# Gathers behind the accumulating transfers, an earlier first expert slot, and another layout of the list operand

## The chip, the cores and the metric

The kernel runs on one core of a Trainium2 chip. What counts is the device time of one execution in microseconds (us), the median of several runs. A profiled execution gives the page and the trace from which every time here is read; all durations are us unless marked ns. The engines are PE (TensorE: PE for matmuls, PEld for its weight loads), DVE (VectorE), ACT (ScalarE), POOL (GpSimd) and SP (SyncE, which here only issues DMAs). "L1404" is line 1404 of the kernel before.

## The reference

The input is an image of 256 channels and 64 x 64 = 4096 tokens. Layer 0 adds a linear attention over windows. Layer 1 adds softmax attention with 8 heads, then a routed feed-forward network with 8 experts of which every token uses two:

```python
# x: (1, 256, 64, 64)
x = x + _L0_conv_ref(_gn(x), Wq, Wk, Wv, Wout, bout)     # linear attention in windows
t = _to_tokens(x)                                        # (1, 4096, 256)
t = t + _L1_attn_ref(_ln_t(t), w_qkv, b_qkv, w_out, b_out)
t = t + _L1_ffn_ref(_ln_t(t), Wr, br, ln_g, ln_b, W1, b1, W2, b2)

# _L1_ffn_ref, xt of shape (4096, 256), 8 experts, hidden size 1024
probs = softmax(xt @ Wr + br)
top_p, top_idx = top_k(probs, 2)
weights = top_p / top_p.sum(-1, keepdims=True)
xe = layernorm(xt) * ln_g[e] + ln_b[e]
y[e] = gelu(xe @ W1[e] + b1[e]) @ W2[e] + b2[e]
out = sum over the two chosen experts e of weight[e] * y[e]
```

## The kernel before

The first part (to about 1105 us) is layer 0 and the projections of queries, keys and values. The change does not touch it.

**Attention (1105 to 2210).** There are 16 rounds, one for each chunk of 512 queries and each half of the heads. Each round runs over 32 key tiles `i`. For a tile, `scores` makes eight score matmuls (L1739) into one PSUM bank (`ps_one`, the first of four heads) and three banks (`ps_three`). ScalarE takes the exponential of the first bank (L1748) and of the three others (L1751) into one of eight SBUF buffers `pe`. `value_sums` multiplies the buffer by the values (L1698). The softmax denominators need the sum of a round's 32 buffers. For most tiles VectorE adds the buffer to a running total (L1770). Seven tiles of a round (i = 5, 9, ... 29; five in the last round) go another way: GpSimd starts an accumulating DMA (L1759) that adds the buffer to a second total. The buffer is free for a later tile once that transfer has landed; the list `free` gives it out again six tiles on. Later in the next round the totals are joined, turned and divided, and `some_projections` (L1673, L1677) makes the output projection of finished tokens.

**Early slots.** The experts work in slots of up to 256 tokens (two units of 128). For four experts the first slot can be filled from the first twelve token tiles, whose routing is done during the attention; the token lists of these early slots, `lists`, come back from DRAM in round 12. A slot has these steps, all in the generator `run`, which yields after each piece so that other work can be laid between the pieces:

- `load`: the weights through SP (`weights`, L1350 to L1375), and for each unit an indirect gather of 128 token rows issued by GpSimd (L1389).
- `enter`: four transposes by TensorE (L1404) into the bank `ps_tp`, and two operations that scale and shift them into `xe`. For the early slots those are ScalarE's (L1409); for the others VectorE's (L1413).
- eight hidden tiles: two matmuls each (L1438) into `ps_hp`, and GELU by ScalarE (L1441).
- for each unit the output product (L1454, eight matmuls into `ps_yp`), an addition of the bias (L1458) and an indirect scatter by GpSimd (L1459).

fp32 matmuls have two records each in the trace, transposes and bf16 matmuls one.

The loop over the attention's tiles calls `next(work_on)` twice in the last round: the first call loads slot 0, the second slot 1. A gather waits for its list and stands in GpSimd's queue where the scheduler put it, which is round 12, among the accumulating transfers. [...]

**End of the attention.** After the last tile the code adds the last denominators (`by_ones` into `den`), copies the last sums (`take`, L1782 on ScalarE), takes four reciprocals (L1894) and products (L1895) on VectorE, and makes the last projections (L1673). The PSUM banks of the attention are then given up, and `route_and_run` opens its own.

**`route_and_run` (L1473 to L1664).** It finishes the routing of all tokens on VectorE while TensorE works on early slots: `advance(n)` takes n pieces of `run`. It counts tokens by expert with two matmuls (L1533, L1534), works out the row of each token in its expert's list, and then inverts these positions into a list of tokens for each slot, by matmuls with one-hot operands. This list stage works on 8 token tiles at a time (`G`), in four groups for the first choice and four for the second. VectorE makes `line` (L1633), the one-hot of the place within a unit, 128 places for each of 8 tiles; and `piece` with three planes for the 72 units (`NPC`): the one-hot of the unit (L1635), that times the token's number (ScalarE, L1636), and that times a tile number `high` (L1637). Eight matmuls (L1639) follow with `line` as weights and the last two planes of `piece` as the moving operand, 144 columns. `line` and `piece` have two buffers each, and one piece of an early slot (`advance(1)`) is laid behind every group. The operand `counter`, 0 to 127 repeated 8 times, is made on GpSimd (L1621), and `high` too (L1629). After the last group VectorE turns the sums into `source` (L1656 on) and the usual slots' gathers can start.

The operands before have the tile index last:

```python
line  = r_work.tile([P, P, G], BF16)          # weights  line[:, :, i]
piece = r_work.tile([P, 3, NPC, G], BF16)     # moving   piece[:, 1:, :, i]
```

so that both operands of a matmul step through SBUF by 8 elements, 16 bytes.

## Time and profile before

| what | us |
|---|---|
| median of 3 runs (2773.73 to 2778.75) | 2773.91 |
| the profiled execution | 2777.12 |
| its span in the trace | 2775.3 |
| mean granted TensorE clock | 0.986 |
| attention, 16 rounds | about 1105 to 2210 |
| four early slots, with the list stage (2252 to 2277) | 2218 to 2290 |
| usual slots | 2290 to 2730 |
| last combination and output | 2730 to 2775 |

How to read it: a timeline row gives the start, the length, the engine, the line, the operation and its operands as output<-input, the shape, the number of instructions, and in brackets the idle time of the engine ahead of it with what ended it. Several like instructions in succession share a row. The DMA queue's own time is not in an engine's row: a transfer issued by GpSimd shows there only with its issue. In the rows by stretch, PEclk is the share of full speed granted to TensorE. Pages of the costliest groups put the attention's matmuls first, with L1739 at 564.2 and 558.0 us and L1698 at 352.5 and 193.9; the experts' products L1438 and L1454 have 249.7 and 241.0. The list's matmuls L1639 have 18.0 in the stretch from 2252 to 2278, in 64 records.

### The profile page before, as it was taken

The page shows a single profiled execution, that of the slowest core. Times are in us where ns is not written, and L with a number is a line of the kernel's source. Part 1 is how long each engine was busy: PE and PEld are TensorE (multiplying, and loading weights), DVE is VectorE, ACT ScalarE, POOL GpSimd, SP SyncE. Part 2 cuts the span into 40 slices and gives each one's busy share as a digit, 9 for nine tenths or more (in the row PEclk, how much of TensorE's full clock was granted, in tenths as well). Part 3 has the DMA queues.
Part 4 walks back from the last instruction along what each step waited for, and adds up shares of the span by engine and source line. Part 5 has one row for each costly group of instructions (what it writes and reads, how often), then busy time and mean ns, then how long its engine had stood idle before and what let it go on. Part 6 is the DMA issues. An engine that isn't in the chain of part 4 may idle for free.

```text
span 2775.3 us, 72311 instructions
## 1 busy us (share of the span) xinstructions
PE 2661.1 (96%) x31106; PEld 1212.8 (44%) x31106; DVE 1873.0 (67%) x2517; ACT 1512.8 (55%) x2110; POOL 822.4 (30%) x918
## 2 busy tenths in 40 slices
PE   6889999988999999999999999999999999999996
PEld 5454336645433655111212121212121278888884
DVE  6758688565878875888888889888788851111114
ACT  3322323222332334999898989898889742222222
POOL 2057777404777741000000100000200012222220
PEclk9999999999999999999999999999999999999996
DMA  5000000000000000555555555555556546565665
GB/s 144 6 23 25 11 28 21 8 12 23 24 11 28 21 21 1 107 111 118 108 120 109 121 112 112 111 112 123 117 109 150 142 132 196 200 208 190 217 207 194
DMA packets 120995, 266.09 MB, mean 96 GB/s; under 512 B 20658, under 2 KB 81816, under 8 KB 106580
## 3 DMA queue, kind: packets, MB, share of 16 engines
q0 software_dynamic: 22368, 133.18, 23.0%
q1 hardware_dynamic: 91124, 119.20, 13.1%
q10 hardware_dynamic: 7168, 8.92, 1.0%
q8 instruction: 248, 4.06, 0.6%
q14 instruction: 87, 0.71, 0.1%
HBM read 127.81 MB, written 18.12 MB: 53 GB/s over the span
## 4 chain that ended last, share of the span: by engine, by line
PE 91%; DMA 3%; DVE 3%; issue 2%; POOL 1%; ACT 0%; ACTq 0%; SPq 0%; DVEq 0%; POOLq 0%
PE ps_three L1739 18%; PE ps_acc L1698 18%; PE ps_hp L1438 8%; PE ps_sc L822 8%; PE ps_yp L1454 8%; PE ps_acc L838 7%; PE ps_sc L722 3%; PE ps_sc L749 3%; PE ps_acc L780 3%; PE ps_two L407 2%; PE ps_two L440 2%; PE ps_mm L1238 2%; DMA yrows<-v,qk 2%; PE ps_two L521 1%; PE ps_acc L768 1%
## 5 line engine op out<-in xcount | busy, mean ns | idle before, releaser
L1739 PE MATMUL ps_three<-qk 32*64 32x512 f32 x6144 | 564.2, 613 | 2.3 <-DVE t L1677 1.3
L1739 PE MATMUL ps_one<-qk 32*64 32x512 f32 x2048 | 558.0, 614 | 5.2 <-ACT pe L1748 5.2
L642 ACT COPY sm<-ps_sc 128x384 f32<-128x384 f32 (+3 forms) x454 | 218.5, 511 | 525.7 <-PE ps_sc L822 338.7
L1770 DVE TENSOR_TENSOR act<-act,pe 128x2048 f32<-128x2048 f32 x195 | 446.8, 2292 | 84.9 <-ACT pe L1751 53.0
L1751 ACT ACTIVATE pe<-ps_three 128x1536 f32<-128x1536 f32 x330 | 477.4, 1447 | 0.0
L649 DVE TENSOR_TENSOR sm<-ps_sc,mask 128x512 f32<-128x512 f32 (+3 forms) x740 | 340.2, 519 | 68.9 <-PE ps_sc L822 65.7
L1770 DVE TENSOR_TENSOR act<-act 128x2048 f32<-128x2048 f32 x150 | 344.9, 2299 | 57.2 <-ACT act L1751 44.0
L649 POOL TENSOR_TENSOR sm<-sm,mask 128x192 f32<-128x192 f32 (+3 forms) x428 | 349.7, 847 | 113.9 <-ACT sm L642 113.6
L1759 POOL DMA_DIRECT2D pe<-pe x108 | 93.1, 862 | 933.1 <-ACT pe L1751 653.5
L1698 PE MATMUL ps_acc<-pe,v 128*32 128x512 f32 x2640 | 352.5, 606 | 0.0
L1441 ACT ACTIVATE v<-ps_hp,qk 128x256 f32<-128x256 f32 (+1 forms) x288 | 133.1, 462 | 343.8 <-PE ps_hp L1438 341.9
L1739 PEld LDWEIGHTS ps_three<-qk 32*64 32x64 f32 x6144 | 112.6, 130 | 415.4 <-ACT pe L1748 243.2
L1751 ACT ACTIVATE act<-ps_three 128x1536 f32<-128x1536 f32 x182 | 263.1, 1446 | 0.0
L1438 PE MATMUL ps_hp<-qk 128*128 128x256 f32 (+1 forms) x1152 | 249.7, 373 | 0.3 <-ACT qk L1409 0.3
L1454 PE MATMUL ps_yp<-qk,v 128*128 128x256 f32 x1088 | 241.0, 379 | 0.0
L822 PE MATMUL ps_sc<-qk 32*64 32x384 f32 (+3 forms) x3584 | 234.5, 458 | 0.1
L1748 ACT ACTIVATE pe<-ps_one 128x512 f32<-128x512 f32 x330 | 197.4, 598 | 66.5 <-PE ps_one L1739 36.1
L649 POOL TENSOR_TENSOR sm<-sm,ycut 128x384 f32<-128x384 f32 (+4 forms) x146 | 147.3, 1029 | 252.3 <-ACT sm L642 252.0
L1438 PEld LDWEIGHTS ps_hp<-qk 128*128 128x128 f32 x1152 | 197.2, 190 | 47.4 <-ACT v L1441 13.1
L1454 PEld LDWEIGHTS ps_yp<-qk,v 128*128 128x128 f32 x1088 | 204.2, 190 | 26.5
L838 PE MATMUL ps_acc<-sm,v 128*32 128x256 f32 (+3 forms) x2688 | 213.2, 419 | 0.1
L1698 PE MATMUL ps_acc<-act,v 128*32 128x512 f32 x1456 | 193.9, 604 | 0.0
(335 smaller groups left out, 2875.4 us busy)
## 6 DMA issues: line engine op xcount, KB each, us to landing
pe<-pe POOLq DMA_DIRECT2D x108, 1024.0 KB, 7.6
qk<-in_L_ffn_W SPq DMA_DIRECT2D x72, 1024.0 KB
by<-recs SPq DMA_DIRECT2D x48, 256.0 KB
qk<-in_L_ffn_b SPq DMA_DIRECT2D x36, 128.0 KB
rows<-in_x SPq DMA_DIRECT2D x16, 256.0 KB
y<-yrows SPq DMA_DIRECT2D x8, 512.0 KB
y<-yrows ACTq DMA_DIRECT2D x8, 512.0 KB
rec<-recs SPq DMA_DIRECT2D x60, 64.0 KB
```

The source lines that it names most:

```text
L642: copied = nc.scalar.copy(sm[:, :used], sc[:, :used])
L649: done = engine.tensor_mul(to, of, mk.unsqueeze(1).to_broadcast(list(to.shape)))
L822: nc.tensor.matmul(scs[h][u : u + rows, at : at + n], kT[hs[h], P * i + u : P * i + u + rows], qT[hs[h], CH * ix + CELL * c0 : CH * ix + C ...
L838: nc.tensor.matmul(acc[hs[h], CELL * c0 : CELL * c1], v[:, i, hs[h]], sms[h][:, at : at + n], start=not begun[0], stop=last and at == plac ...
L1438: nc.tensor.matmul(hp[:, :n], w1[:, k, tok(m)], x_now[:, k, :n], start=k == 0, stop=k == KC - 1)
L1441: done["gelu"] = nc.scalar.activation(hid[:, m, :n], hp[:, :n], AF.Gelu, bias=cols[:, m : m + 1]).ins
L1454: product = nc.tensor.matmul(yp, hid[:, m, tok(j)], w2[:, m, :], start=m == 0, stop=m == NH - 1)
L1698: nc.tensor.matmul(to[D * hd : D * (hd + 1), :], lhsT(hd), rhs(hd), start=start, stop=stop, skip_group_check=True,)
L1739: nc.tensor.matmul(to[CELL * u : CELL * (u + 1), :], qk[hs, 1, g, P * i + CELL * u : P * i + CELL * (u + 1)], qk[hs, 0, g, chunk(qc)], sta ...
L1748: first = nc.scalar.activation(head(pe, 0), one, AF.Exp, scale=C**-0.5)
L1751: nc.scalar.activation(pe[:, CH:], three.rearrange("p h n -> p (h n)"), AF.Exp, scale=C**-0.5).ins
L1770: latest[:] = [nc.vector.tensor_add(total, total, weights_of[r, i]).ins]
```

## The change

It has three parts.

1. `load` orders its gathers behind the transfer that was issued last when the code of the load stands there. `scores` keeps that transfer as `done["moved"]`. `issue_after` is an order within one engine's queue and adds no wait for an end. The gathers of slot 0 then stand between the last transfer of round 14 and the first of round 15; those of slots 1 and 2 stand behind the last transfer of all, ahead of `counter`; those of slot 3 stand behind `units` and `high`.
2. `run` has one more `yield`, after the `enter` of the first slot, and a parameter `bank` for the PSUM bank of that first `enter`. The attention passes a `ps_one` bank and calls `next(work_on)` once more ahead of the reciprocals and the last projections. In TensorE's queue the four transposes of slot 0 come before the last eight L1673 projections, and the `enter` of slot 1 comes behind the sixteen L1438 of slot 0, instead of ahead of them. A GELU of a single element is issued on ScalarE right behind the last `take`, so that the table of the function is loaded there.
3. `piece` has the units last, and a new bf16 operand `units` (a copy of 0 to 71 made on GpSimd) takes the place of `counter` in L1635. The moving operand of a matmul is then 72 elements in succession, twice. In L1635 and L1637 the values by tile (`which`, `high`) are repeated along the innermost dimension. `line` stays as it was.

In TensorE's queue the number of instructions stays the same. Behind the list's groups of eight stand 2, 3, 4, 3, 3 expert matmuls, then 1 with four transposes and one L1454, then three L1454; before it was 2, 3, 2, 2, 3, 4, and the transposes with one L1454. Twelve L1454 and sixteen L1438 follow before the first usual slot's transposes (before: fifteen and sixteen). ScalarE and GpSimd have one operation more each. Two other users of `run`, in branches that aren't taken here, are adapted in the same manner and left out below.

```diff
-        def run(slots, slot_ps, beside, done):
+        def run(slots, slot_ps, beside, done, bank):
...
-                for q in slot[1:]:
-                    xs.append(next_of("xs"))
-                    nc.gpsimd.indirect_dma_start(
...
+                with tc.issue_after(done["moved"]) if "moved" in done else nullcontext():
+                    for q in slot[1:]:
+                        xs.append(next_of("xs"))
+                        nc.gpsimd.indirect_dma_start(
...
-            def enter(of, by_scalar):
+            def enter(of, by_scalar, tp):
...
-                tp = ps.tile([P, KC, SLOT], F32, tag="tp", name="ps_tp")
...
             ahead.append(load(slots[1]))
             yield
+            xe = enter(ahead[0], slots[0][0] is not None, bank().rearrange("p (k n) -> p k n", k=KC))
+            yield
             (ps,) = slot_ps
-            xe = enter(ahead[0], slots[0][0] is not None)
...
                 if after:
-                    xe = enter(ahead[0], after[0] is not None)
+                    tp = ps.tile([P, KC, SLOT], F32, tag="tp", name="ps_tp")
+                    xe = enter(ahead[0], after[0] is not None, tp)
...
+                    units = r_work.tile([P, NPC], BF16, name="units", bufs=1)
+                    nc.gpsimd.tensor_copy(units, iota[:, :NPC])
...
-                            piece = r_work.tile([P, 3, NPC, G], BF16, name="piece")
-                            nc.vector.tensor_tensor(piece[:, 0], some(which, NPC), counter[:, :NPC], ALU.is_equal)
+                            piece = r_work.tile([P, 3, G, NPC], BF16, name="piece")
+                            on_units = lambda v: v[:, i8 : i8 + G].unsqueeze(2).to_broadcast([P, G, NPC])
+                            nc.vector.tensor_tensor(
+                                piece[:, 0], on_units(which), units.unsqueeze(1).to_broadcast([P, G, NPC]), ALU.is_equal
+                            )
                             nc.scalar.activation(piece[:, 1], piece[:, 0], AF.Copy, scale=cst["number"])
-                            nc.vector.tensor_mul(piece[:, 2], piece[:, 0], some(high, NPC))
+                            nc.vector.tensor_mul(piece[:, 2], piece[:, 0], on_units(high))
...
-                                    piece[:, 1:, :, i],
+                                    piece[:, 1:, i, :],
...
-                        nc.gpsimd.dma_start(buffers[sums_of[r, other]], pe, accum_op=ALU.add)
+                        moving = nc.gpsimd.dma_start(buffers[sums_of[r, other]], pe, accum_op=ALU.add)
+                        done["moved"] = moving.ins
...
-                work_on = run(usual, slot_ps, beside, done)
+                first_bank = lambda: ps.tile([P, CH], F32, tag="one", name="ps_one")
+                work_on = run(usual, slot_ps, beside, done, first_bank)
...
-                take(last, nc.scalar.copy)
+                with tc.issue_after(take(last, nc.scalar.copy).ins):
+                    gelu = work.tile([1, 1], F32, name="gelu")
+                    nc.scalar.activation(gelu, ident[:1, :1], AF.Gelu)
                 by_ones(den, buffers[sums_of[last, own]], False, True)
+                next(work_on)
                 rec = work.tile([P, CH], F32, tag="rec", name="rec")
```

More of the change, by code (lines that the diff above doesn't have):

```diff
@@ L1386, in load @@
                 xs = []
-                for q in slot[1:]:
-                    xs.append(next_of("xs"))
-                    nc.gpsimd.indirect_dma_start(
-                        out=xs[-1],
-                        out_offset=None,
-                        in_=zrows[:n, :],
-                        in_offset=bass.IndirectOffsetOnAxis(ap=rows[:, q : q + 1], axis=0),
-                    )
+                with tc.issue_after(done["moved"]) if "moved" in done else nullcontext():
+                    for q in slot[1:]:
+                        xs.append(next_of("xs"))
+                        nc.gpsimd.indirect_dma_start(
+                            out=xs[-1],
+                            out_offset=None,
+                            in_=zrows[:n, :],
+                            in_offset=bass.IndirectOffsetOnAxis(ap=rows[:, q : q + 1], axis=0),
+                        )
                 return *of, xs
-            def enter(of, by_scalar):
+            def enter(of, by_scalar, tp):
                 *_, cols, xs = of
                 n = P * len(xs)
-                tp = ps.tile([P, KC, SLOT], F32, tag="tp", name="ps_tp")
                 for j in range(len(xs)):
@@ L1633, in route_and_run @@
                             made = nc.vector.tensor_tensor(line, some(within, P), counter, ALU.is_equal)
-                            piece = r_work.tile([P, 3, NPC, G], BF16, name="piece")
-                            nc.vector.tensor_tensor(piece[:, 0], some(which, NPC), counter[:, :NPC], ALU.is_equal)
+                            piece = r_work.tile([P, 3, G, NPC], BF16, name="piece")
+                            on_units = lambda v: v[:, i8 : i8 + G].unsqueeze(2).to_broadcast([P, G, NPC])
+                            nc.vector.tensor_tensor(
+                                piece[:, 0], on_units(which), units.unsqueeze(1).to_broadcast([P, G, NPC]), ALU.is_equal
+                            )
                             nc.scalar.activation(piece[:, 1], piece[:, 0], AF.Copy, scale=cst["number"])
-                            nc.vector.tensor_mul(piece[:, 2], piece[:, 0], some(high, NPC))
+                            nc.vector.tensor_mul(piece[:, 2], piece[:, 0], on_units(high))
                             for i in range(G):
@@ L1956, in tile_conv_attn_hybrid @@
                     all_of(ops)
-            slot_ps, beside, done = [], [], {}
-            work_on = run(usual, slot_ps, beside, done)
-            next(work_on)
-            next(work_on)
+                slot_ps, beside, done = [], [], {}
+                work_on = run(usual, slot_ps, beside, done, one_bank)
+                for _ in range(3):
+                    next(work_on)
             route_and_run(work_on, slot_ps, beside, done)
@@ L1967, in tile_conv_attn_hybrid @@
         ):
-            for _ in run([(None, q) for q in range(USUAL, NU)], [ps], [], {}):
+            one_bank = lambda: ps.tile([P, KC * SLOT], F32, tag="tp", name="ps_tp")
+            for _ in run([(None, q) for q in range(USUAL, NU)], [ps], [], {}, one_bank):
                 pass
```

## The prediction

> **What bounds the kernel now.** I read the page's first, second and fourth parts first: they ask which engine sets the end and where it pauses.
>
> ```profile
> PE 2661.1 (96%) x31106; PEld 1212.8 (44%) x31106; DVE 1873.0 (67%) x2517; ACT 1512.8 (55%) x2110; POOL 822.4 (30%) x918
> ...
> PE 91%; DMA 3%; DVE 3%; issue 2%; POOL 1%; ACT 0%; ACTq 0%; SPq 0%; DVEq 0%; POOLq 0%
> ```
>
> TensorE is busy 96% of the span and is 91% of the chain of waits. So an edit pays only where it fills a pause of TensorE, raises its granted clock, or shortens its own stream. The three parts of the change stand at three places: round 12 of the attention (about 1972 us), the passage from attention to experts (2205 to 2231), and the list stage (2252 to 2277). I looked at each alone. First the sums over stretches (length, busy time of each engine, granted clock, DMA share); the first two rows run from a round's first transfer to the next round's, two rounds apart in work of the same kind, the second with round 12's stall; the last two are from the passage.
>
> ```profile
> 1796.65:1863.17 66.52, 66.52 (x780) 12.92 (x776) 59.09 (x42) 62.66 (x66) 6.02 (x7) 1.00 0.57 116
> 1935.32:2010.46 75.14, 70.14 (x783) 13.33 (x776) 58.03 (x34) 62.50 (x66) 15.77 (x12) 0.95 0.57 120
> 2220.00:2225.00 5.00, 2.72 (x12) 1.85 (x12) 4.52 (x19) 2.51 (x4) 4.22 (x6) 0.93 0.29 82
> 2225.00:2230.00 5.00, 5.00 (x18) 4.06 (x17) 4.69 (x13) 2.44 (x6) 0.00 (x0) 0.73 0.10 28
> ```
>
> With the same instructions on TensorE (776 weight loads) round 12 is 8.62 longer, has 5.0 of idle time and a lower clock, and GpSimd (the fifth engine) is busy for 15.77 instead of 6.02. The timeline of GpSimd there:
>
> ```profile
> 1971.69 2.44 POOL L1389 DMA_INDIRECT qk<-zrows,lists  x1 [8.69 <-DMA rec<-recs]
> 1974.43 2.02 POOL L1389 DMA_INDIRECT qk<-zrows,lists  x1 [0.30 <-issue]
> 1976.75 2.04 POOL L1389 DMA_INDIRECT qk<-zrows,lists  x1 [0.30 <-issue]
> 1979.10 3.06 POOL L1389 DMA_INDIRECT qk<-zrows,lists  x1 [0.30 <-issue]
> 1982.17 1.02 POOL L1759 DMA_DIRECT2D pe<-pe  x1
> ```
>
> Four gathers hold the queue, the accumulating transfer behind them starts at 1982.17 and lands 7.12 later in the chain; the exponential that wants its buffer is this one:
>
> ```profile
> 1989.37 0.60 ACT L1748 ACTIVATE pe<-ps_one 128x512 f32<-128x512 f32 x1 [6.20 <-DMA pe<-pe]
> ```
>
> The passage, TensorE's timeline:
>
> ```profile
> 2214.81 2.02 PE L1673 MATMUL ps_three<-wo,act 128*128 128x264 f32 x8 [0.36 <-DVE act L1895]
> 2217.74 1.06 PE L1404 MATMUL ps_tp<-cst,qk 128*128 128x128 f32 x8 [0.91 <-PE ps_three L1673]
> 2219.07 1.99 PE L1438 MATMUL ps_hp<-qk 128*128 128x256 f32 x8 [0.27 <-ACT qk L1409]
> 2222.59 0.41 PE L1404 MATMUL ps_tp<-cst,qk 128*128 128x128 f32 x2 [1.53 <-DMA qk<-zrows,lists]
> 2223.75 0.44 PE L1404 MATMUL ps_tp<-cst,qk 128*128 128x128 f32 x2 [0.75 <-DMA qk<-zrows,lists]
> 2224.03 7.03 PE L1438 MATMUL ps_hp<-qk 128*128 128x256 f32 x24
> ```
>
> Here the first expert product waits for eight transposes and ScalarE's copies, then TensorE waits for a gather, and the next 24 records take 7.03 instead of 5.2 (32 take 7.07 later), at clock 0.73. The list stage: the early list's matmuls in the attention first, then a group of the late list's, then the weight loads of all 64 (min/median/max ns):
>
> ```profile
> 1879.36 1.62 PE L1105 MATMUL ps_three<-qk 128*128 128x16 bf16 x24
> 1880.83 2.03 PE L1673 MATMUL ps_three<-wo,act 128*128 128x264 f32 x8
> ...
> 2252.48 2.25 PE L1639 MATMUL ps_acc<-piece,line 128*128 128x144 bf16 x8
> 2254.55 0.61 PE L1438 MATMUL ps_hp<-qk 128*128 128x256 f32 x2
> ...
> L1639 PEld LDWEIGHTS <-line x64: 142/146/152, 2252.3 to 2276.4; 128*128 128x128 bf16 x64
> ```
>
> Eight take 2254.55 - 2252.48 = 2.07, so 0.259 each. That is a strange pace: a transpose of 128 columns in fp32 goes every 0.115 (four from 2274.00 to 2274.46).
>
> **What the skill says.** "SBUF — State Buffer", section Specifications (TRN2): lines of 16 bytes, at least two hits on a line for full bandwidth, each cross to a new line pays. The moving operand before takes every eighth bf16, a step of 16 bytes, so every element is a new line; 0.259 agrees with a price but no row isolates it. "VectorE: DVE Perf Modes", What auto-detection actually checks: the doubled mode wants 16-bit operands with step one, so an innermost broadcast should drop the two `piece` operations to single pace. Before they run 452 and 456 ns for 576 elements, the `line` operation 692 for 1024: slope 0.536 ns an element, 0.144 fixed; no row shows them at single pace. "ScalarE: Activation LUTs", What ACT_TABLE_LOAD costs: about 1283 ns; the trace has 1.28. "TensorE: Matmul & The Clock Gate", What's actually happening: an idle window of about 3.4 us halves the clock; the 0.73 above fits.
>
> **Part 1, the gathers.** Removed from round 12: the wait of four gathers. ScalarE's cadence is 2.04 us a tile there; from the exponential at 1981.23 three tiles on would be 1987.35, and the tile stands at 1996.01: **-8.7**. Cross-check: the stretches above, 75.14 - 66.52 = 8.6. Of it 5.0 is TensorE's idle time, the rest its slow restart. Bounds -6 (if another wait is just behind) to -9. Added: two gathers after round 14's last transfer (2134.24), before round 15's first (2147.48). GpSimd is idle there for 12.38; at 2.0 to 2.4 each they need 4.8: nothing. If that cover failed it would again be up to 8.7. The other four come after the last transfer (2185.63), in 28.71 of idle time; slot 2's wait for the first slot's transposes, and behind them on GpSimd stand two memsets, `counter`, `units` and slot 3's gathers, all wanted only at 2237 or later.
>
> **Part 2, the first slot.** Four transposes and two ScalarE copies of slot 0 go into a `ps_one` bank ahead of the last projections. TensorE idles 1.39 there waiting for VectorE's reciprocals, so the four (0.46) are hidden. The GELU table load (1.28) goes to 2209.8, where ScalarE idles till 2218.45; the tiny activation is hidden with it. The first expert product then needs only the banks that the last projection's add frees at 2217.64 on VectorE: it starts at 2217.74. From there 32 records take 6.90 (as 2238.67 to 2245.57 in the same timeline), slot 1's transposes 0.5, and 0.8 for ScalarE's four L1507 (0.59 each) that now stand before a copy, an estimate of what TensorE sees of their 2.4: the first L1454 at 2226.0 instead of 2230.90, **-4.9**. No wait for a gather (-2.28), no cold clock (-1.8) and eight transposes less in front make up most of it. The weights' loads on SP keep their place: only the gathers of a load are ordered anew. Slot 2's four transposes then move behind that (+0.46), so the list stage starts **4.4** earlier. Range -2.5 (clock still drops in 2210:2218, with less work then) to -6. The pieces are ready by about 2250.4, 2.1 ahead of 2252.48; they follow from the counts' matmuls, which move earlier with TensorE, so they do not become late.
>
> **Part 3, the list's layout.** 64 matmuls at 0.259. With a contiguous moving operand: lower bound 0.065, near the pace of the early list's 24 matmuls ((1880.83 - 1879.36) / 24 = 0.061, with 16 moving columns and weights strided too, so a strided weight load doesn't set 0.259); upper bound 0.146, the weight load's row as it stands; and no gain at all if the stride isn't the cause. I take 0.09, between. 64 x (0.259 - 0.09) = **-10.8**, bounds -7.2 to -12.4, or 0. The `piece` operations at single pace: 0.144 + 576 x 1.04 ns = 0.744 (an estimate from the slope doubled), 16 x 0.29 = 4.7 us on VectorE. Per group VectorE then needs about 2.0 (0.61 for `line`, 0.70 and 0.74 for the two `piece` operations, from start to start), TensorE 0.72 for the list and 1.1 to 1.3 of expert matmuls between. Two groups are built ahead; I see no wait that lasts, but the cover is thin. If it goes, about 0.2 a group, some 1 us. `units` costs GpSimd 0.2, hidden. After the list the first usual slot's gather must land before its transposes at 2290.35; between the last list matmul and them TensorE has 12.1 us of work instead of 13.4 (12 instead of 15 products of L1454, then 16 of L1438), and the slack before was about 1.5: just covered.
>
> **Sum.** -8.7 - 4.4 - 10.8 = -23.9. The profiled execution took 2777.12 (span 2775.3), so 2753.2; it lies 3.2 above the median of the runs shown, 2773.91, and within their spread; carried to the median 2750.0.
>
> **Rivals.**
> 1. The list stage keeps its pace (the weight load sets it, or VectorE at single pace makes each group wait). For: no row shows the contiguous form; VectorE's cover is thin. Against: 0.06 for the early list. Gain of part 3 only 0 to 4: 2757 to 2761.
> 2. Part 2 is lost: the product starts when the banks come free anyway, and the cold clock stays. For: the gap at 2217.74 is put down to a bank. Against: two waits for a gather are gone. Gain 0 to 1.5: 2753 to 2755.
> 3. The stall returns in its new place: a gather before round 15's first transfer waits for its list and the transfer lands late. Gain of part 1 only 0 to 3: 2756 to 2759. Against: 12.38 idle.
> 4. Slower: the throttle. With its pauses gone TensorE draws without rest, and the granted clock falls. Place: all of the chain that is TensorE's. Price: 0.01 of the mean clock (0.986 now) is 0.91 x 2775 / 100 = 25 us. It decides from 0.976 (no change), and 0.973 gives 2781. Against: the low clocks before stand only behind pauses.
>
> **How the numbers follow.** The forecast, all three parts, 2745 to 2755: 58%. Rival 1: 17%. Rival 2: 13%. Rival 3: 5%. Rival 4: 4%. Several losses together, no change: 3%. About 0.2% (5.5 us) is what a measurement can tell from no change. Faster 0.93, same 0.03, slower 0.04. The range 2744 to 2761 holds the forecast and most of rivals 1 to 3.
>
> **What would show it.** Right: no exponential waits for `pe<-pe` in round 12 and its stretch reads 1.00; the first L1438 stands directly behind L1673, with no wait for a gather and no clock below 0.9 till 2230; a group of eight L1639 takes about 0.7; L1635 and L1637 take about 0.74; the mean clock stays at 0.986 or above. Wrong: a group that still takes 2 us, TensorE waiting for `piece` or `line`, an exponential waiting in round 15, or TensorE waiting for the gather of the first usual slot near 2275.

## The result and the profile after

The changed kernel takes 2756.49 us (median of 4 runs, 2753.76 to 2761.25) beside 2774.11 for the kernel before (4 runs, 2773.73 to 2778.75): a ratio of 0.9935, 95% interval 0.9917 to 0.9952, or 17.6 less. The prediction was 2750.0 with a range of 2744 to 2761. The profiled execution took 2761.25 with a span of 2759.4, beside 2775.3 before.

The line numbers in a run's rows are those of that run's own kernel. In the changed kernel L1405, L1410, L1440, L1443 and L1457 are L1404, L1409, L1438, L1441 and L1454 of before (transposes, copies, hidden tiles, GELU, output products); L1681, L1685 and L1908 are L1673, L1677 and L1895 (last projections, their addition, products with the reciprocals); L1641, L1645 and L1647 are L1635, L1637 and L1639 (the list); L1391, L1756, L1759 and L1767 are L1389, L1748, L1751 and L1759 (gathers, exponentials, accumulating transfers). In the other runs they lie a few lines away.

The three places look as the prediction wanted them. First the sums over stretches: round 10 and round 12, each from its first transfer to the next round's, and two stretches of the passage (length, busy time of PE, PEld, DVE, ACT, POOL, then clock, DMA share, GB/s).

```profile
1804.37:1870.90 66.53, 66.53 (x780) 12.90 (x776) 59.10 (x42) 62.64 (x66) 6.02 (x7) 1.00 0.57 116
1943.03:2009.46 66.43, 66.43 (x784) 12.89 (x776) 58.03 (x34) 62.48 (x66) 6.03 (x8) 1.00 0.61 128
2220.00:2225.00 5.00, 4.55 (x23) 3.50 (x22) 4.49 (x17) 3.56 (x9) 0.00 (x0) 1.00 0.01 2
2225.00:2230.00 5.00, 5.00 (x26) 4.43 (x25) 4.22 (x12) 1.76 (x5) 2.37 (x3) 1.00 0.76 218
```

Round 12 takes 66.43 instead of 75.14, without idle time, and the clock stays at 1.00 in the passage, where it read 0.73. GpSimd's timeline shows the first two gathers in their new place, between the last transfer of one round and the first of the next:

```profile
2132.96 0.86 POOL L1767 DMA_DIRECT2D pe<-pe  x1 [8.49 <-ACT pe L1756]
2134.12 1.07 POOL L1391 DMA_INDIRECT qk<-zrows,lists  x1 [0.30 <-issue]
2135.50 2.02 POOL L1391 DMA_INDIRECT qk<-zrows,lists  x1 [0.30 <-issue]
2146.49 0.99 POOL L1767 DMA_DIRECT2D pe<-pe  x1 [8.97 <-ACT pe L1759]
```

The gathers end at 2137.5 and GpSimd still waits 8.97 for the exponential: nothing is late behind them. TensorE's timeline through the passage:

```profile
2209.76 0.66 PE L1405 MATMUL ps_one<-cst,qk 128*128 128x128 f32 x4
2210.25 0.61 PE L1681 MATMUL ps_three<-wo,act 128*128 128x264 f32 x2
2211.86 1.60 PE L1681 MATMUL ps_three<-wo,act 128*128 128x264 f32 x6 [1.00 <-DVE act L1908]
2213.88 2.02 PE L1681 MATMUL ps_three<-wo,act 128*128 128x264 f32 x8 [0.41 <-DVE act L1908]
2216.96 6.30 PE L1440 MATMUL ps_hp<-qk 128*128 128x256 f32 x28 [1.07 <-DMA cstm<-in_constants]
2223.71 1.13 PE L1440 MATMUL ps_hp<-qk 128*128 128x256 f32 x4 [0.45 <-ACT v L1443]
2224.68 0.60 PE L1405 MATMUL ps_tp<-cst,qk 128*128 128x128 f32 x4
2225.12 7.07 PE L1457 MATMUL ps_yp<-qk,v 128*128 128x256 f32 x32
```

The first transposes fill a part of TensorE's wait for the reciprocals, and no gather is waited for any more. The wait of 1.07 ahead of the first L1440 is put down to a load of `cstm`, but the chain of waits has that load landing at 2217.45, after the product began at 2216.96. The last two additions L1685, which free a bank, run from 2215.93 to 2216.70, and in e8 below the same wait is put down to them. So the bank that the prediction named is the likelier cause; no run separates them. The list stage, in the same timeline:

```profile
2247.14 0.67 PE L1647 MATMUL ps_acc<-piece,line 128*128 128x144 bf16 x8
2247.65 1.07 PE L1440 MATMUL ps_hp<-qk 128*128 128x256 f32 x4
```

A group of eight takes 2247.65 - 2247.14 = 0.51 instead of 2.07. The price on VectorE is close to the 0.744 that was estimated (rows by line and form, busy time and mean ns; the first two before, the others after):

```profile
L1637 DVE TENSOR_TENSOR piece<-piece,high 128x576 bf16<-128x576 bf16 x8 | 3.6, 456 | 0.3
L1635 DVE TENSOR_TENSOR piece<-which,counter 128x576 bf16<-128x576 bf16 x8 | 3.5, 452 | 0.0
L1645 DVE TENSOR_TENSOR piece<-piece,high 128x576 bf16<-128x576 bf16 x6 | 4.5, 757 | 0.2
L1641 DVE TENSOR_TENSOR piece<-which,units 128x576 bf16<-128x576 bf16 x6 | 4.5, 751 | 0.0
```

The two spans differ by only 15.9, although these stretches give more. Differences of start times in the two timelines say why: the first score matmul of the attention stands at 1102.81 before and at 1108.93 after, 6.1 later, in code that the change does not touch. From there to the end it is 1672.49 before and 1650.50 after, 22.0 less. In the trace after, the granted clock also reads 0.50 for 3.41 early in the attention (from 1113.92), and from the first score matmul to round 12 it takes 834.10 instead of 832.51.

### The profile page after: what moved, and what is told of

It is laid out like the page before. It is cut to its first block, busy times and chain, and to the rows that moved or that the text cites. A ratio compares the mean times of both kernels' runs of the same rounds, so it can differ in the third digit from the quotient of the medians.

```text
span 2759.4 us, 72312 instructions
## 1 busy us (share of the span) xinstructions
PE 2649.4 (96%) x31106; PEld 1207.4 (44%) x31106; DVE 1877.0 (68%) x2517; ACT 1511.5 (55%) x2111; POOL 819.3 (30%) x919
## 4 chain that ended last, share of the span: by engine, by line
PE 91%; DVE 3%; DMA 3%; issue 2%; ACT 0%; POOL 0%; ACTq 0%; DVEq 0%; SPq 0%; POOLq 0%
PE ps_three L1747 19%; PE ps_acc L1706 18%; PE ps_sc L822 8%; PE ps_yp L1457 8%; PE ps_hp L1440 7%; PE ps_acc L838 7%; PE ps_sc L722 3%; PE ps_sc L749 3%; PE ps_acc L780 3%; PE ps_two L407 2%; PE ps_two L440 2%; PE ps_mm L1238 2%; DMA yrows<-v,qk 2%; PE ps_two L521 1%; PE ps_acc L768 1%
## 5 line engine op out<-in xcount | busy, mean ns | idle before, releaser
L1759 ACT ACTIVATE pe<-ps_three 128x1536 f32<-128x1536 f32 x330 | 477.4, 1447 | 0.0
L1767 POOL DMA_DIRECT2D pe<-pe x108 | 93.1, 862 | 938.3 <-ACT pe L1759 645.7
L1443 ACT ACTIVATE v<-ps_hp,qk 128x256 f32<-128x256 f32 (+1 forms) x288 | 132.8, 461 | 344.2 <-PE ps_hp L1440 342.3
L1759 ACT ACTIVATE act<-ps_three 128x1536 f32<-128x1536 f32 x182 | 263.2, 1446 | 0.0
L1440 PE MATMUL ps_hp<-qk 128*128 128x256 f32 (+1 forms) x1152 | 248.5, 371 | 1.9 <-DMA cstm<-in_constants 1.1
L1457 PE MATMUL ps_yp<-qk,v 128*128 128x256 f32 x1088 | 241.2, 379 | 0.0
L1756 ACT ACTIVATE pe<-ps_one 128x512 f32<-128x512 f32 x330 | 197.3, 598 | 60.3 <-PE ps_one L1747 35.9
L1440 PEld LDWEIGHTS ps_hp<-qk 128*128 128x128 f32 x1152 | 195.2, 189 | 48.5 <-ACT v L1443 16.0
L1457 PEld LDWEIGHTS ps_yp<-qk,v 128*128 128x128 f32 x1088 | 203.8, 190 | 26.2
```

What stands on the lines that cost most here:

```text
L1440: nc.tensor.matmul(hp[:, :n], w1[:, k, tok(m)], x_now[:, k, :n], start=k == 0, stop=k == KC - 1)
L1443: done["gelu"] = nc.scalar.activation(hid[:, m, :n], hp[:, :n], AF.Gelu, bias=cols[:, m : m + 1]).ins
L1457: product = nc.tensor.matmul(yp, hid[:, m, tok(j)], w2[:, m, :], start=m == 0, stop=m == NH - 1)
L1756: first = nc.scalar.activation(head(pe, 0), one, AF.Exp, scale=C**-0.5)
L1759: nc.scalar.activation(pe[:, CH:], three.rearrange("p h n -> p (h n)"), AF.Exp, scale=C**-0.5).ins
```

## The experiments

In the table each stretch is the difference of two start times: **attention starts** at the first score matmul; **round 12** is from its first transfer to the next round's; **passage** is from the last matmul with `ones` to the first list matmul; **list** is from there to the transposes of the first usual slot (which holds the early slots' matmuls laid between and behind the groups, too); the mean is over the timed and profiled runs of that kernel, with their standard deviation.

| kernel | attention starts | round 12 | passage | list | mean of runs (n, s.d.) |
|---|---|---|---|---|---|
| before | 1102.81 | 75.14 | 42.26 | 37.87 | 2775.0 (48, 4.5) with e1 to e4 |
| after | 1108.93 | 66.43 | 37.90 | 26.47 | |
| e1 after again | 1104.34 | 66.43 | 37.87 | 26.54 | 2757.4 (6, 2.9) |
| e2 part 1 alone | 1106.62 | 66.43 | 40.91 | 37.93 | 2771.7 (22, 1.7) |
| e3 part 2 alone | 1108.13 | 71.98 | 37.82 | 37.91 | 2775.5 (22, 4.1) |
| e4 part 3 alone | 1104.77 | 73.47 | 42.40 | 26.98 | 2766.9 (11, 2.7) |
| e5 without part 1 | 1103.79 | 75.19 | 37.87 | 26.72 | 2759.2 (6, 4.9) |
| e6 two gathers | 1102.16 | 68.47 | 37.84 | 26.41 | 2754.4 (6, 0.6) |
| e7 step of 8 bytes | 1104.12 | 66.43 | 37.77 | 29.77 | 2757.5 (4, 1.6) |
| e8 two hidden tiles early | 1101.16 | 66.43 | 36.09 | 26.69 | 2752.8 (6, 1.7) |
| e9 e8 and step of 4 bytes | 1107.73 | 66.42 | 36.09 | 27.51 | 2758.2 (6, 3.4) |
| e10 no early GELU | 1108.36 | 66.43 | 37.59 | 26.81 | 2757.6 (4, 3.3) |
| e11 before | 1101.89 | 71.96 | 42.35 | 37.84 | |
| e12 before | 1105.79 | 73.57 | 42.32 | 37.88 | |

The kernel before had a mean of 2777.2 (11 runs, 5.2) beside e5 to e8 and 2776.3 (11, 4.2) beside e9 to e12.

**e1, the change again.**

> The changed kernel once more, for more runs and a second trace. In the first pair of traces the attention of the changed kernel begins 7.7 us later than before, in code that the change does not touch, and from there to the end it is 23.6 us shorter (2775.3 - 2759.4 + 7.7). Theory 1, the first 1105 us vary from run to run: the start of the attention falls anywhere within some 8 us in the traces to come, whatever the kernel; the stretch from the attention's first score matmul to the end is again 23 to 24 us shorter than before; the medians differ by 18 to 24 us (ratio 0.9915 to 0.9935). Theory 2, the change costs 6 to 8 us in the first part: this trace begins the attention late again, as do those of the single parts, and the medians stay at -17.6 (0.9935 to 0.994).

(The 7.7 of the expectation was taken at the attention's first transfer, behind the 3.41 at half clock; at the first score matmul it is 6.1.) The attention starts at 1104.34 this time, and from there the trace takes 1649.25, 23.2 less than the first trace of before. The median is 2757.88, ratio 0.9937 (0.9921 to 0.9952). Over all fourteen traces the start lies between 1101.2 and 1108.9: the kernel before has 1102.81, 1101.89 and 1105.79, the changed one 1108.93 and 1104.34. So a pair of spans can be wrong by several us, and single stretches are the better witness. That half of theory 1 holds; the ratio, though, lies just outside its range and inside theory 2's, and theory 2 is not refuted. What the totals lack against the traces is taken up below.

**e2 to e4, each part alone on the kernel before.** The diffs are the hunks of the change: for e2 those of `load` and of `done["moved"]`, for e3 those of `run`, `enter`, the GELU and `next(work_on)`, for e4 those of `units` and `piece`.

> Part 1 alone (the gathers' order), on the kernel before. By the prediction: round 12 takes 66.4 to 66.6 from its first transfer to the next round's instead of 75.1, no exponential waits for a transfer of pe<-pe there; the passage and the list stage as before. Ratio 0.9965 to 0.9973 (-7.5 to -9.5 us). Rival, the stall comes back before round 15 or another wait stands behind it: less than -3 us, ratio above 0.999, and an exponential waits for pe<-pe in round 12 or 15.

Round 12 takes 66.43, and no exponential waits for a transfer there or in round 15. The passage keeps its waits for gathers:

```profile
2213.19 1.06 PE L1405 MATMUL ps_tp<-cst,qk 128*128 128x128 f32 x8 [0.91 <-PE ps_three L1674]
2214.52 1.99 PE L1439 MATMUL ps_hp<-qk 128*128 128x256 f32 x8 [0.27 <-ACT qk L1410]
2218.36 0.41 PE L1405 MATMUL ps_tp<-cst,qk 128*128 128x128 f32 x2 [1.84 <-DMA qk<-zrows,lists]
2219.54 0.44 PE L1405 MATMUL ps_tp<-cst,qk 128*128 128x128 f32 x2 [0.77 <-DMA qk<-zrows,lists]
2219.81 5.34 PE L1439 MATMUL ps_hp<-qk 128*128 128x256 f32 x24
```

(The 24 records take 5.34 instead of 7.03: the half clock did not fall here this time.) So the mechanism is as predicted. But the runs give a ratio of only 0.9986 (0.9978 to 0.9994), where 0.9965 to 0.9973 was expected: 3.9 less, not 8.7. They also scatter far less than those of before (1.7 against 4.5), and their lowest is the same, 2767.62 beside 2767.72.

> Part 2 alone (first slot's transposes ahead of the last projections, GELU table early), on the kernel before. By the prediction: from the last projection's last matmul to the first output product of slot 0 about 9 us instead of 14, the list stage begins 4.4 us earlier against the end of the attention; round 12's stall stays at 8.6. Ratio 0.998 to 0.9987. Rival, the gain needs the gathers of part 1 (slot 2's gathers late in the queue): less than -2 us, and TensorE waits for zrows again between 2215 and 2226.

The passage takes 37.82, 4.4 less, to the tenth what was predicted, and needs nothing of part 1. The ratio is 1.0003 (0.9993 to 1.0013): the 0.998 to 0.9987 that was expected lies outside the interval. The 4.4 of the trace are missing in 22 runs, and scatter alone doesn't account for that.

> Part 3 alone (units last in the list operand), on the kernel before. By the prediction as it now stands: a group of eight list matmuls takes about 0.52 instead of 2.07, the two piece operations 0.75 instead of 0.45, and the first usual slot's transposes come 11 to 12.5 us earlier against the start of the list stage. Ratio 0.9952 to 0.9963. Rival, VectorE at its longer operations cannot keep up when the early slots are in the order of before (2, 3, 2, 2 matmuls between the groups instead of 2, 3, 4, 3): TensorE waits for line or piece by some 0.3 to 0.6 in each of five groups, and the gain is 8 to 10 us.

The list stretch takes 26.98 instead of 37.87, 10.9 less, just short of the 11 to 12.5 expected, and the ratio is 0.9969 (0.9957 to 0.998), short of 0.9952 to 0.9963. It is 0.5 longer than in the changed kernel. Of the rival's five waits the trace has one, of 0.32 for `piece` ahead of the third group. Alone, the parts shorten their stretches by 8.7, 4.4 and 10.9; together by 8.7, 4.4 and 11.4 (first pair of traces).

**e5 and e6, the stall of round 12.** e5 is the changed kernel with the hunk of `load` undone. e6 leaves slot 0's two gathers where they were:

```diff
-                with tc.issue_after(done["moved"]) if "moved" in done else nullcontext():
+                with tc.issue_after(done["moved"]) if "moved" in done and slot[0] != 0 else nullcontext():
```

> The changed kernel with part 1 undone: the four gathers of slots 0 and 1 stand in round 12 again, parts 2 and 3 stay. The traces so far give every stretch to within 0.6 us whatever the run, but for two: the start of the attention (1102.8 to 1108.9) and round 12 where the gathers stand in it (75.14, 73.47 and 71.98, against 66.43 three times where they don't). Theory A, the stall of round 12 is drawn anew in every run, from 0 to 12 us, and the profiled run of before had a large one: this kernel is 3 to 6 us slower than the changed one in the mean (2760 to 2763 against 2757), and its runs scatter more (standard deviation 4 or more, as 4.5 for before and 4.1 for part 2 alone, against 1.7 for part 1 alone and 2.9 for the change). Theory B, the stall is about 8.6 always and part 1 gives 4 to 5 us back elsewhere: 2765 to 2767, and scatter as small as that of the changed kernel.

The mean is 2759.2, with runs from 2754.46 to 2766.84 and a deviation of 4.9. The scatter is theory A's, and the mean is far below theory B's 2765. But it is below theory A's 2760 to 2763 too: only 1.8 above e1, on another chip, and 4.8 above e6, on the same chip but with two gathers still in round 12. Six runs are few, so what part 1 is worth inside the changed kernel is known only roughly.

> The changed kernel with the two gathers of slot 0 left in round 12 and the other four in their new place. Before, the transfer behind the gathers started 10.6 us later than the cadence of its neighbours (1982.17 against about 1971.5) and the loss was 8.66, so some 2 us are slack. If the stall is only how late that transfer starts, two gathers less (2.0 and 3.1, with a pause of 0.3 each: 5.7) leave a loss of 3 in a run in which four would have cost 8.66, and nothing in most runs: round 12 takes 66.4 to 69.5, the mean is 2756 to 2758.5. Rival, it is the wait for the list that holds the queue and the number of gathers matters little: 70 or more in round 12, and the mean of the runs as without part 1.

The round takes 68.47, a loss of 2.0, within the range. All six runs lie within 2753.31 to 2754.85; their mean, 2754.4, is below the 2756 to 2758.5 expected. GpSimd's queue and the one wait that is left on ScalarE:

```profile
1971.08 2.44 POOL L1391 DMA_INDIRECT qk<-zrows,lists  x1 [8.65 <-DMA rec<-recs]
1973.83 2.02 POOL L1391 DMA_INDIRECT qk<-zrows,lists  x1 [0.30 <-issue]
1975.84 1.04 POOL L1767 DMA_DIRECT2D pe<-pe  x1
```

```profile
1992.91 0.60 ACT L1756 ACTIVATE pe<-ps_one 128x512 f32<-128x512 f32 x1 [0.51 <-DMA pe<-pe]
```

Counted from the round's first transfer, the one behind the gathers starts at 41.1 (1975.84 - 1934.72) instead of 46.9 (1982.17 - 1935.32) in the first trace of before. That is 5.7 earlier, and the exponential's wait falls by as much, from 6.20 to 0.51. The stall is the lateness of that transfer less some slack; the wait for the list is the same in both and is not the cause.

**e7 and e9, the step of the moving operand.** e7 keeps four tiles innermost, e9 two; `units` is not made, and e9 has e8's edit as well.

```diff
-                            piece = r_work.tile([P, 3, G, NPC], BF16, name="piece")
+                            S = 4
+                            piece = r_work.tile([P, 3, G // S, NPC, S], BF16, name="piece")
...
-                                    piece[:, 1:, i, :],
+                                    piece[:, 1:, i // S, :, i % S],
```

> The changed kernel with the list operand laid out as 2 x 72 x 4: the moving operand steps by 4 elements, 8 bytes,[...] and VectorE's operations have four tiles innermost with step one; units is not made. Theory 1, the price of the layout before was a new line for every element: with two reads a line the matmuls keep their new pace, a group of eight in 0.50 to 0.55. Theory 2, any step costs in proportion: 8 bytes is half of 16, a group takes about 1.2 to 1.3. On VectorE: 0.45 for a piece operation if step one innermost is what its faster mode wants, 0.75 if the short inner run spoils it. The whole time: same as the changed kernel within 0.5 us by theory 1, 5 to 6 us longer by theory 2.

Theory 2. A group at a step of 8 bytes:

```profile
2240.66 1.24 PE L1651 MATMUL ps_acc<-piece,line 128*128 128x144 bf16 x8
2241.71 1.05 PE L1440 MATMUL ps_hp<-qk 128*128 128x256 f32 x4
```

1.05 for eight (2241.71 - 2240.66), half of 2.07 and twice 0.51, though less than the 1.2 to 1.3 expected. The weight operand `line` has its step of 16 bytes in all of these kernels, so the moving operand alone sets the pace. VectorE's operations are back at 451 and 458 ns. The list stretch is 3.2 longer than the change's 26.5; 64 x (0.131 - 0.064) = 4.3 would be due to the matmuls, and the 5 to 6 of the expectation was too much. The runs, on another chip than e1's, don't show it at all (mean 2757.5 beside 2757.4).

> The kernel of e8 with the list operand as 4 x 72 x 2: the moving operand steps by 2 elements, 4 bytes, and VectorE has two tiles innermost with step one. So far a list matmul took 0.259 at a step of 16 bytes, 0.131 at 8 and 0.064 at 2. Theory 1, the time is in proportion to the bytes stepped over until something else is the floor: 4 bytes give 0.065, which is the floor of the contiguous form already, a group 0.52; VectorE's piece operations take 0.45, not 0.75. Theory 2, any step but one doubles the time, whatever its length between 4 and 8 bytes: 1.05 a group. The list stage then is bound by VectorE and ScalarE rather than TensorE (0.69 + 0.45 + 0.46 a group): list start to the first usual slot's transposes 25 to 26.8 by theory 1 (26.5 in the changed kernel), 29 to 30 by theory 2. Whole: like e8, or up to 1.5 less by theory 1.

Theory 1 for TensorE, and a miss in the rest: a group takes 0.56, the multiplication 456 ns, but the comparison L1645 stays at 703 (it reads `counter` in pairs 16 bytes apart, which the multiplication does not; whether that operand or the operation makes the difference was not separated). And the stretch is 27.51, longer than the changed kernel's 26.5. The timeline shows a wait that was not expected:

```profile
2261.90 7.07 PE L1443 MATMUL ps_hp<-qk 128*128 128x256 f32 x32
2270.26 0.41 PE L1405 MATMUL ps_tp<-cst,qk 128*128 128x128 f32 x2 [1.29 <-DMA qk<-zrows,qk]
2271.50 0.44 PE L1405 MATMUL ps_tp<-cst,qk 128*128 128x128 f32 x2 [0.83 <-DMA qk<-zrows,qk]
```

Without the 1.29 it would be 26.2. The first usual slot's gather comes too late. It is issued at 2264.32, 7.4 after its list is ready (L974 at 2256.77). Before that, SP's queue has this:

```profile
2259.65 0.37 SPq L1364 DMA_DIRECT2D qk<-crows  x1
2260.11 0.38 SPq L1517 DMA_DIRECT2D zrows<-act  x1
```

The last rows of `zrows` are ready at 2255.6 (ScalarE's last L1513, 2255.03 and 0.60 long), but their store stands in SP's queue behind a load of `crows`, and that stands behind seven reads of expert numbers into SP's registers (`values_load` in `weights`, L1354). The chain of waits has these from 2254.84 to 2259.4, some 0.56 from one to the next and one of 1.2. So SP's reads hold the store for most of the time, rather than the load of `crows`. The gather starts 4.2 after the store. The changed kernel has the same picture, store at 2263.38 and gather at 2267.58, and there the gather lands just in time (the four transposes at 2273.61 take 0.85 instead of 0.60). The same row of reads stands there, from 2258.11 to 2262.6. e1, e4 and e8 have pauses of 0.44, 0.65 and 0.43 within the same transposes, put down to the gather in e8. That an earlier store would help was read from this order; no run moves it.

**e8, two hidden tiles earlier.** `run` takes the first two hidden tiles of slot 0 from `bank` too, the attention calls `next(work_on)` three times, and `route_and_run` advances by 7 instead of 9.

```diff
+                    if slot is slots[0] and m < soon:
+                        hp = bank()
+                    else:
+                        (ps,) = slot_ps
+                        hp = ps.tile([P, SLOT], F32, tag="hp", name="ps_hp")
...
-                next(work_on)
+                for _ in range(3):
+                    next(work_on)
```

> The changed kernel with the first two hidden tiles of slot 0 (four L1438) put into ps_one banks too, between the last projections, where TensorE stands idle for 1.0, 0.41 and 1.07 in the traces of the change; their GELU follows there. From the last sum of the denominators to the first output product it takes 7.72 + 8.12 = 15.9 in the changed kernel. If only TensorE's idle time is filled: 14.0 to 14.6, and the list stage begins 1.3 to 1.9 earlier; the mean of the runs falls by as much, which the scatter hides (ratio 0.9931 to 0.9935). Rival, the projections are late by what is put ahead of them, so that routing (chosen) is late for the counts: no gain or a loss of up to 1, and TensorE waits for chosen at L1533's place.

From the last denominators to the first output product it takes 14.07 instead of 15.9, and the passage is 1.8 shorter. The hidden tiles stand in TensorE's pauses:

```profile
2202.15 1.13 PE L1443 MATMUL ps_one<-qk 128*128 128x256 f32 x4 [0.66 <-ACT qk L1410]
2203.12 1.05 PE L1684 MATMUL ps_three<-wo,act 128*128 128x264 f32 x4
2204.01 1.03 PE L1443 MATMUL ps_one<-qk 128*128 128x256 f32 x4
2204.87 2.39 PE L1684 MATMUL ps_three<-wo,act 128*128 128x264 f32 x10
2208.22 5.44 PE L1443 MATMUL ps_hp<-qk 128*128 128x256 f32 x24 [0.95 <-DVE t L1688]
```

The median is 2752.90, ratio to before 0.9914 (0.9895 to 0.9934), the lowest of all kernels tried. The ratio owes something to the kernel before, which was slower beside these runs than beside e1 to e4; against the change, the 1.8 of the stretch is what is shown. With the operand of e9 it is no better: that kernel's runs have a mean of 2758.2.

**e10, without the early GELU** (the operation and its order behind `take` taken out, so that the first GELU is slot 0's).

> The changed kernel without the one-element GELU behind the last copy. Theory 1, the table load needs no operand and stands directly behind ScalarE's copies of slot 0 (L1410), which end 5 us or more before the first hidden tile is ready: nothing is lost, first L1440 to first L1457 8.1 as before, and the copies come 1.3 earlier. Theory 2, the load runs only when its activation could: the first GELU is 1.28 later, and TensorE, with two banks for hidden tiles, waits up to 1.28 for it; 9 to 9.5.

ScalarE's timeline settles how the load behaves, and TensorE's what it costs:

```profile
2217.81 1.28 ACT L1443 ACT_TABLE_LOAD   x1 [6.66 <-PE ps_hp L1440]
2219.10 0.84 ACT L1443 ACTIVATE v<-ps_hp,qk 128x256 f32<-128x256 f32 x2
```

```profile
2216.64 1.97 PE L1440 MATMUL ps_hp<-qk 128*128 128x256 f32 x8 [1.07 <-DMA cstm<-in_constants]
2218.44 1.04 PE L1405 MATMUL ps_tp<-cst,qk 128*128 128x128 f32 x8
2219.63 5.45 PE L1440 MATMUL ps_hp<-qk 128*128 128x256 f32 x24 [0.15 <-ACT v L1443]
```

The load did wait for the activation's operand, theory 2, though ScalarE had been idle for 6.66. Yet the first L1440 to the first L1457 takes 8.28 instead of 8.1: the order of the queue is another one, the eight transposes of slots 1 and 2 stand behind the fourth hidden-tile matmul (eight records) and fill the wait, and only 0.15 is seen. The whole passage is even 0.3 shorter, 37.59. The early GELU moves the load as intended, and in this trace nothing is lost without it; but the scheduler's other order came with the edit, so what it is worth in the order of the changed kernel was not measured.

**e11 and e12, the kernel before again.**

> The kernel before once more, for a second trace of its round 12. Its 48 timed runs beside e1 to e4 lie from 2767.7 to 2784.3, with part 1 alone 2767.6 to 2775.4. If the stall is drawn anew in each execution, this trace may show a round 12 of 66.4 to 70 as well as one of 72 to 76; its start of gathers (36.4 after the round's first transfer in four traces) and the length of the fourth gather (0.95 or 3.06) tell which of the two is drawn.

> The same as e11, a third trace of the kernel before: round 12 anywhere from 66.4 to 76 if the stall is drawn anew, 72 to 76 again if every profiled execution has it and only the timed ones vary.

71.96 and 73.57. The gathers start 36.4 after the round's first transfer every time, and the rows of e11 differ from those of the first trace in the last gather:

```profile
1975.91 2.04 POOL L1389 DMA_INDIRECT qk<-zrows,lists  x1 [0.30 <-issue]
1978.26 0.96 POOL L1389 DMA_INDIRECT qk<-zrows,lists  x1 [0.30 <-issue]
1979.22 1.02 POOL L1759 DMA_DIRECT2D pe<-pe  x1
```

The fourth gather takes 0.96 here and 3.06 in the first trace, and the exponential then waits 3.88 instead of 6.20. Which length it takes goes with VectorE. Its additions L1770 that begin nearest to the fourth gather are these, in the first trace and in e11:

```profile
1979.05 2.29 DVE L1770 TENSOR_TENSOR act<-act,pe 128x2048 f32<-128x2048 f32 x1 [1.07 <-ACT pe L1751]
1978.39 2.29 DVE L1770 TENSOR_TENSOR act<-act,pe 128x2048 f32<-128x2048 f32 x1 [1.27 <-issue]
```

In the first trace the gather starts at 1979.10, 0.05 after the addition, and ends 0.82 after the addition has ended; in e11 it starts at 1978.26, 0.13 ahead of it, and is through in 0.96. All the early slots' gathers of the attention fit: of the 58 that the fourteen traces have between 1900 and 2204, the 42 that start during such an addition end 0.8 to 1.1 after it, and the 16 others take 0.95 to 1.07. So what differs from trace to trace is who comes first in a race of 0.2. No run moves the additions, so this is read from the traces and not tried.

The rest of the loss goes with the clock, which behind the stall reads 0.50 for 3.41 or for 6.83. The losses against 66.43 fall into three pairs: the long gather with 6.83 gives 8.71 and 8.76 (before, e5), the short one with 6.83 gives 7.04 and 7.14 (e4, e12), the short one with 3.41 gives 5.55 and 5.53 (e3, e11). None of the six traces has a small stall; that timed runs had one is not shown.

## Why the prediction was right, and where it was off

- **The sum: inside the range, in part by luck.** The measured 2756.5 is 6.5 above the 2750.0 forecast and above the forecast's own band of 2745 to 2755. By the number alone it would stand for rival 3 (2756 to 2759, the stall returns in round 15), but no exponential waits for a transfer there. The range was drawn for the rivals; what filled it is something else, as follows.
- **Part 1, the mechanism: right; the size: too large.** "-8.7" was taken from one profiled execution, one of the two largest of the six traces with four gathers in round 12, whose mean loss is 7.1. That is 1.6 too much. In the timed runs part 1 alone is worth 3.9 (interval 1.7 to 6.1).
- **What the runs lack beyond that is not part 1's alone, and its cause is open.** Against the stretches of the traces (with the mean loss of 7.1 in round 12), the means of e1 to e4, e9 and e10 gain 2.6 to 5.7 less than they should, each with an error of 1.5 to 4. e3 and e4, which keep the stall, lack 4.9 and 2.6. The means of e5 to e8, on another chip, lack nothing. The starts of the attention go the same way: in the seven other traces of edited kernels it lies at 1104.3 to 1108.9 (mean 1107.0), in e5 to e8 at 1101.2 to 1104.1 (mean 1102.8), in the three traces of the kernel before at 1101.9 to 1105.8 (mean 1103.5). So theory 2 of e1, some us lost in the first part, fits these figures best. It is not shown: the timed runs don't tell their start of the attention, and why an edit further on should move it is unknown. The kernel before may also have stalls smaller than any traced: the shortest stall and the earliest start of all traces would put it at 2772.8 (e11's 2773.52, begun 0.7 earlier), and 19 of its 48 runs are below, down to 2767.7.
- **Part 2: right in size.** 4.4 predicted; 42.26 - 37.90 = 4.4 measured in the trace (the runs of e3 don't show it). e3 has it with the gathers left in round 12, so it is the new order of the transposes in TensorE's queue, and nothing of part 1, that ends the wait for a gather. The first expert product started 0.2 later than predicted against the last denominators (7.7 instead of 7.5), ScalarE held TensorE for 0.45 where 0.8 was estimated.
- **Part 3: right, 0.6 more than predicted.** -10.8 predicted from 0.09 a matmul; they took 0.064, the lower bound. 64 x (0.259 - 0.064) = 12.5 would be due, 37.87 - 26.47 = 11.4 came. Of the difference 0.36 is a wait for ScalarE's GELU between two groups; the rest is in pauses too short for the timeline to list. VectorE's 0.75 was estimated as 0.744; the slope of 0.536 ns doubled would be 1.07, not 1.04, and give 0.761, as close from the other side. Its cover held, with hardly a gap in VectorE's queue. The cover for the first usual slot's gather, "just covered", was a little short: the four transposes at 2273.61 take 0.25 more than elsewhere, with a pause of 0.44 in e1.
- **Rival 4's price** has a slip of its own: 0.973 instead of 0.986 at 25 us for each 0.01 gives 2782 to 2783, not 2781. The mean clock stayed at 0.986.
- **The Trainium skill's rule on lines** ("SBUF — State Buffer", Specifications (TRN2): at least two hits on a line for full bandwidth) pointed to the right edit but not to the right law: at a step of 8 bytes, two hits on each line, e7's matmul takes 0.131, twice the contiguous form. The measurement decides.

## What to carry to other kernels

A stall read from one trace can be a draw: before it is priced, see whether it has parts that vary and what they race with (here the last gather with VectorE's addition, and the clock behind both), and take the mean of several executions. In a queue that serves two masters, put the work that has no hurry behind the work that frees buffers. Where kernels scatter by more than an edit is worth, compare the same stretch in two traces. But add the stretches up and hold the sum against the runs: here they agree on one chip and differ by some us on others.

## What the runs showed of the hardware

- A list matmul's time (128 x 128 weights, 144 moving columns, bf16) follows, down to a floor, the bytes stepped over by its moving operand: 0.259 at 16 bytes, 0.131 at 8, 0.069 at 4 (0.56 for eight), 0.064 at 2. The first two are 144 x 16 / 259 = 8.9 and 144 x 8 / 131 = 8.8 bytes a ns; at 4 bytes that law would give 0.065, which is about the floor that the contiguous form shows, so these two don't tell law and floor apart.
- VectorE's comparison with only two elements innermost took 703 ns, the multiplication beside it 456; with four both took about 455, with one repeated value innermost 751 and 757. Step one innermost was not enough for the comparison with two.
- GELU's table load of 1.28, ahead of an activation whose operand was late, did not start while ScalarE stood idle for 6.66, but only when the operand was there (e10).
- GpSimd served its queue in order: the accumulating transfer behind four gathers started at 1982.17, as the fourth ended, and with two gathers fewer 5.7 earlier against its round (e6).
- An indirect gather of 128 rows that started while VectorE ran an addition of 128x2048 fp32 (2.29) held GpSimd until 0.8 to 1.1 after the addition's end, 1.07 to 3.18 in all; otherwise it took 0.95 to 1.07 (58 gathers between 1900 and 2204 in fourteen traces).
- A stall of the same length left the clock at 0.50 for 3.41 in some traces and for 6.83 in others (an exponential's wait of 3.88 in e3 and e11, and in e4 and e12).
- SP, which here does more than issue DMAs, took about 0.56 for each expert number that it read into its registers, and its DMAs stood behind these reads (e9, seven from 2254.84 to 2259.4).
